# Where the feed-forward's last additions run, and when the third pair's tables are spread: a two-layer attention hybrid on one core

## The chip, the cores and the metric

The kernel runs on one core of one Trainium2 chip. A core has five engines that run side by side, each with its own queue of instructions: TensorE (PE, with PEld for its weight loads) multiplies matrices into PSUM, VectorE (DVE) and ScalarE (ACT) do elementwise work and can read PSUM, GpSimd (POOL) does elementwise work between SBUF tiles, and SyncE (SP) only starts transfers. Transfers (DMAs) are also started from POOL's queue. An instruction waits in its queue until the semaphores it needs have been raised by other engines or by transfers.

The metric is the device time of one execution in microseconds (us); lower is better. Beside it stands the span of a profiled execution, from its first to its last instruction.

## The reference

The input is x, eight images of 32 x 32 positions with 384 channels in fp32. In short:

```python
# layer 0: six heads of 64; scores get two tables of relative positions
x = x + conv_attention(group_norm(x))
#   attn = softmax(q * 64**-0.5 @ k.T + rel_h[:, :, :, :, None] + rel_w[:, :, :, None, :])
#   rel_h = einsum('bhwc,hkc->bhwk', q, Rh),  rel_w = einsum('bhwc,wkc->bhwk', q, Rw)
# layer 1 on the 1024 tokens of an image, one causal head of 384
t = t + causal_attention(layer_norm(t))
# feed-forward, weights reduced to signs, 384 -> 1536 -> 384
t = t + ffn(layer_norm(t))

def quantize(ag):        # one group of images; at both ends of the feed-forward
    gamma = jnp.max(jnp.abs(ag))
    return jnp.clip(ag * QB / (gamma + EPS), -QB + EPS, QB - EPS)     # QB = 128, EPS = 1e-5
```

With eight images and five groups a group is one image, and images 5, 6 and 7 belong to no group: their feed-forward output is zero, so only images 0 to 4 compute it. What the change touches is the last clip with the addition to t behind it, and the way in which the tables rel_h and rel_w reach the score products.

## The kernel before

**Images one after the other.** The loop in `run` takes the images in the order 5, 0, 1, 2, 3, 4, 6, 7. For each it traces layer 0 (`layer0`, with `products` and `attend0_fast`), then layer 1 (`attention1`), then, for images 0 to 4, the feed-forward `ffn`. Neighbouring images overlap: while the feed-forward of one image ends, q of the next is already multiplied (`project_qk`, L505). The last additions of a feed-forward and the output transfers are packed into a function `finish`, put on the list `unfinished`, and called inside the next image's `products`. So there are five joins where a feed-forward's end meets the next image's products: those into images 1, 2, 3, 4 and 6. The joins into images 0 and 7 have none, and image 5 opens the kernel.

**The end of the feed-forward.** The tile y has eight column groups j of 128 x 384. VectorE adds the bias (L1159) and takes maxima (L1160). `absmax_scale` makes one maximum per partition (L1068), POOL takes it over the partitions (`partition_all_reduce`, L1070), and VectorE adds EPS to it (ga, L1071), takes the reciprocal (L1073) and multiplies by 128 (s, L1074). POOL then goes over y: y times s, cut from above (L1164, eight instructions). In `finish` it cuts y from below (L1168) and adds it to xt, the residual (L1169), eight times each; four output transfers follow on POOL's queue (L1224).

**The products of an image.** Three pairs of heads are computed. `queries_keys(m)` copies q of pair m out of PSUM with a bias, one half by ScalarE (L648) and one by VectorE (L646). `positions(p)` multiplies q of pair p with the position tables into four PSUM banks (f_rel, L505), copies them to two pages of SBUF (L666 on ScalarE, L667 on VectorE), writes each page to DRAM (L673) and reads it back in another order into the tile `near` (L678, four reads for each page), all on SP. k and v are made by two `ProductSet`s of fifteen products each, in six PSUM banks A to F (f_pr), whose partial sums ScalarE keeps in pages (L566, L570) and VectorE combines (L585, and L728 for k and L732 for v). All these matmuls are chained by `in_turn`, so TensorE does them in the order of the text.

`place(p)` splits the table of pair p into a rounded part (L693 on ScalarE) and the rest (L703 on VectorE), and then lays both out as the rows f_r that the score products read: sixteen transfers (L708), eight from `pages[0]` on SP and eight from `pages[1]` on POOL. `place(0)` is called in `products`; `place(1)` and `place(2)` come later, from `attend0_fast`.

**The scores.** In `attend0_fast` each pair of heads and each half of the queries has eight rounds of score products: L804 (q times k) and L808 (f_r times `unit`, which adds the positions) go to PSUM, ScalarE takes the exponential (L814), VectorE adds up (L819, L821), and L829 multiplies with v.

**What sets the order.** TensorE's order in the products and scores is written out by hand. On the other engines a planner in the tile framework puts the instructions in a queue order before the kernel runs: it goes through them with estimated durations and takes, whenever an engine is free, the first in the text's order whose inputs it believes to be ready. `tc.issue_after(ins)` makes the instructions of a block on the engine of `ins` stand behind it. PSUM has eight banks of 128 x 512 (`o_tile`), and large SBUF tiles come from pools of ten images and twelve pages: a tile's first write waits for the last reader of whatever held its place.

Of the kernel before, what the change touches and what calls it, by code (L numbers as in the profile page):

```python
# [11 lines left out]
F32 = mybir.dt.float32  # L12
# [3 lines left out]
ALU = mybir.AluOpType  # L16
# [3 lines left out]
P = 128  # L20
# [5 lines left out]
NPAIR = NH // 2  # L26
# [5 lines left out]
QB, QEPS = 128.0, 1e-5  # L32
# [59 lines left out]
def conv_attn_hybrid(  # L92
# [19 lines left out]
    nc = tc.nc  # L112
# [51 lines left out]
    def weight_forms(pools, eng, raw, s):  # L164
# [49 lines left out]
        out=maskT, in_=maskT, compare_op=ALU.is_ge, fill=MASKED, base=0, pattern=[[1, P]], channel_multiplier=-1  # L214
# [13 lines left out]
    for low in (True, False):  # L228

        nc.gpsimd.affine_select(  # L230
            out=over_group, in_=over_group, compare_op=ALU.is_ge, fill=0.0, base=0 if low else NP_GN - 1,
# [142 lines left out]
    def stages(pools):  # L374
# [238 lines left out]
        def layer0(b, xT):  # L613
# [7 lines left out]
            def r(part, p):  # L621
                if not pools.fast:
                    if part not in rooms:
                        rooms[part] = pools.image(f"r_{b}_{part}", F32R)
                    return rooms[part][:, p, :]
                i, at = divmod(4 * (p % 2) + part, NPAIR)
                if i not in rooms:
                    rooms[i] = pools.flat(f"r_{b}_{i}", F32R)
                return rooms[i][:, ts(at, T)]
# [3 lines left out]
            def queries_keys(m):  # L633
                p = m % NPAIR
                bias = bqk[:, m : m + 1]
                made = ahead.pop((b, m)) if (b, m) in ahead else project_qk(b, xT, m, plain[0])
                for half, ps in enumerate(made):
                    t = ts(half, 512)
                    if m < NPAIR:
                        dst = q[:, p, t]  # L640
                    else:
                        dst = k[:, p, t].rearrange("d (g n i) -> d g i n", n=2, i=P)
                        ps = ps.rearrange("d (g i n) -> d g i n", n=2, i=P)
                    scale = qscale if m < NPAIR else 1.0
                    if half and not (pools.fast and b == ORDER[0]):
                        nc.vector.tensor_scalar(dst, ps, scale, bias, ALU.mult, ALU.add)  # L646
                    else:
                        nc.scalar.activation(dst, ps, AF.Identity, bias=bias, scale=scale)  # L648
# [2 lines left out]

            def positions(p):

                room = pools.flat(f"far_{b}_{p}")
                *pages, near = (room[:, ts(i, T)] for i in range(3))
                for half in range(2):
                    ps = [pools.o_tile(f"rel_{b}_{p}_{half}_{par}") for par in range(2)]
                    for par in range(2):  # L660
                        (in_turn if pools.fast else nc.tensor.matmul)(
                            ps[par], rel[rows[par]].rearrange("d a n -> d (a n)"), q[rows[par], p, ts(half, 512)],
                            start=True, stop=True,
                        )
                    for par in range(2):
                        nc.scalar.copy(pages[par][:HD, ts(half, 512)], ps[par][:HD])  # L666
                        nc.vector.tensor_copy(  # L667
                            pages[par].rearrange("i (w h) -> i w h", h=H)[HD:, :, ts(half, H // 2)],
                            ps[par][HD:].rearrange("i (h w) -> i w h", w=W),
                        )  # L670
                for par in range(2):
                    far = store.tile([P, T], F32, tag=f"far_{p}_{par}", bufs=2, name=f"{pools.path}_far_{b}_{p}_{par}")
                    nc.sync.dma_start(out=far, in_=pages[par])  # L673
                    start = far[0:1, 0:1]
                    for d in range(2):
                        for half in range(2):
                            at, step = (d * HD + (half if d else 16 * half)) * T, (2 if d else 1) * T
                            nc.sync.dma_start(  # L678
                                out=near[ts(4 * d + 2 * half + par, 16)].rearrange("m (n o) -> m n o", n=32),
                                in_=bass.AP(start.tensor, start.offset + at, [[step, 16], [T + 32, 32], [1, 32]]),  # L680
                            )
                return near, [page.bitcast(F32R) for page in pages]

            def behind_of(ins):
                return contextlib.nullcontext() if ins is None else tc.issue_after(ins)
# [9 lines left out]
            def place(p, near, pages, behind=(None, None), rounded=False):  # L695

                for d in range(2):
                    hi, lo, src = both(near, pages, d)
                    if not rounded:
                        with behind_of(behind[0]):  # L700
                            round_off(d, near, pages)
                    with behind_of(behind[1]):
                        nc.vector.tensor_tensor(lo, src, hi.bitcast(F32), ALU.subtract)  # L703
                for part in range(4):
                    for d in range(2):
                        for i in range(2):
                            half = part % 2 if d else part // 2
                            (nc.gpsimd if i else nc.sync).dma_start(  # L708
                                out=r(part, p).bitcast(F32).rearrange("(m i) t -> i m t", i=4)[2 * i + d],
                                in_=pages[i][ts(2 * d + 1 - half, 32)].bitcast(F32),  # L710
                            )

            v = pools.flat(f"v0_{b}")[:, : NJ * C].rearrange("p (j c) -> p j c", j=NJ)

# [19 lines left out]
            near = []  # L734

            def products():

                forms = xf.pop(b)
                of_k, of_v = (ProductSet(b, s, forms) for s in (1, 2))
                for m in range(NPAIR):  # L740
                    queries_keys(m)
                    if m:
                        near.append(positions(m - 1))
                of_k.run(5, put_keys)
                near.append(positions(NPAIR - 1))
                if unfinished:
                    unfinished.pop()()
                for d in range(2):
                    of_k.run(3)
                    with behind_of(of_k.last_copy):  # L750
                        of_k.behind = round_off(d, *near[0])
                of_k.run(N_PROD - of_k.at)
                place(0, *near[0], (None, of_k.last_final), rounded=True)
                early = pools.small.tile([P, 1], F32, tag="early", name=f"early0_{b}")
                with behind_of(of_k.last_copy):
                    of_v.behind = nc.scalar.activation(early, of_k.part["n5"][:, 0:1], AF.Exp, scale=0.0).ins
                of_v.run(N_PROD, put_values)
# [307 lines left out]
        def absmax_scale(am, name):  # L1065

            g = pools.small.tile([P, 1], F32, tag="qg", name=f"qg_{name}")
            nc.vector.tensor_reduce(g, am, AX.X, ALU.max)  # L1068
            ga = pools.small.tile([P, 1], F32, tag="qa", name=f"qa_{name}")
            nc.gpsimd.partition_all_reduce(ga, g, P, bass_isa.ReduceOp.max)  # L1070
            nc.vector.tensor_scalar_add(ga, ga, QEPS)  # L1071
            s = pools.small.tile([P, 1], F32, tag="qs", name=f"qs_{name}")
            nc.vector.reciprocal(s, ga)  # L1073
            nc.vector.tensor_scalar_mul(s, s, QB)  # L1074
            return s, ga
# [13 lines left out]
        def ffn(xt, b, gn):  # L1089
# [40 lines left out]
            s, _ = absmax_scale(am.rearrange("p i n -> p (i n)"), f"1_{b}")  # L1130
# [13 lines left out]
            y = pools.flat(f"y2_{b}")[:, : NJ * C].rearrange("p (j c) -> p j c", j=NJ)  # L1144
            am2 = pools.small.tile([P, NJ], F32, tag="am2", name=f"am2_{b}")
            for j in range(NJ):
# [7 lines left out]
                if j == 4:  # L1154
                    xt = pools.flat(f"xagain_{b}")[:, : NJ * C].rearrange("p (j c) -> p j c", j=NJ)
# [2 lines left out]
                    nc.tensor.matmul(ps[:, :C], h, w, start=(i == 0), stop=(i == len(products) - 1))  # L1158
                nc.vector.tensor_tensor(y[:, j, :], ps[:, :C], b2_sb, ALU.add)  # L1159
                nc.vector.tensor_reduce(am2[:, j : j + 1], y[:, j, :], AX.X, ALU.max, apply_absolute_value=True)  # L1160
            s, _ = absmax_scale(am2, f"2_{b}")

            for j in range(NJ):
                nc.gpsimd.tensor_scalar(y[:, j, :], y[:, j, :], s, QB - QEPS, ALU.mult, ALU.min)  # L1164

            def add():
                for j in range(NJ):
                    nc.gpsimd.tensor_scalar_max(y[:, j, :], y[:, j, :], QEPS - QB)  # L1168
                    nc.gpsimd.tensor_tensor(xt[:, j, :], y[:, j, :], xt[:, j, :], ALU.add)  # L1169
                return xt  # L1170

            yield add
# [2 lines left out]
        unfinished = []  # L1175
# [59 lines left out]
    with ExitStack() as scope:  # L1235
        pools = Pools(scope, tc, "f")
# [43 lines left out]
```

## Time and profile before

| What | us |
|---|---|
| median of 3 runs | 2418.41 (2416.07 to 2419.2) |
| the profiled execution, its time | 2416.14 |
| its span, first to last instruction | 2414.4 |
| PE busy | 2327.5 (96%) |
| PEld busy | 1347.2 (56%) |
| DVE busy | 1518.0 (63%) |
| ACT busy | 1090.6 (45%) |
| POOL busy | 566.8 (23%) |

The mean granted TensorE clock is 0.983 of full speed. Busy time is a sum over stages with different limits, and a matmul counts as busy until its modelled end, so PE's 96% doesn't say that every stage is bound by TensorE. The groups of instructions that the change concerns, as mean duration of one in ns and busy time in us over the whole kernel:

| Group | count | mean ns | busy us |
|---|---|---|---|
| L1164 POOL y times s, cut from above | 40 | 1561 | 62.0 |
| L1168 POOL y cut from below | 40 | 1286 | 50.9 |
| L1169 POOL y added to xt | 40 | 1217 | 48.0 |
| L1224 POOL issue of an output transfer | 20 | 771 | 15.4 |
| L708 POOL issue of rows f_r | 192 | 535 | 102.2 |
| L646 DVE copy of q | 21 | 747 | 15.7 |
| L667 DVE copy of f_rel | 96 | 692 | 61.3 |
| L703 DVE rest of the tables | 48 | 1749 | 84.0 |

In the views, a line gives an instruction or a group with what it wrote and read; in square brackets or behind a bar stands how long its engine had been idle before it, and which engine or transfer ended that. A transfer's line is the time of its issue on its queue; it lands some microseconds later (median 3.0 us for rows issued on SP, 4.0 for rows issued on POOL).

### The profile page before, as it was taken

The page shows a single profiled execution, that of the slowest core. Times are in us where ns is not written, and L with a number is a line of the kernel's source. Part 1 is how long each engine was busy: PE and PEld are TensorE (multiplying, and loading weights), DVE is VectorE, ACT ScalarE, POOL GpSimd, SP SyncE. Part 2 cuts the span into 40 slices and gives each one's busy share as a digit, 9 for nine tenths or more (in the row PEclk, how much of TensorE's full clock was granted, in tenths as well). Part 3 has the DMA queues.
Part 4 walks back from the last instruction along what each step waited for, and adds up shares of the span by engine and source line. Part 5 has one row for each costly group of instructions (what it writes and reads, how often), then busy time and mean ns, then how long its engine had stood idle before and what let it go on. Part 6 is the DMA issues. An engine that isn't in the chain of part 4 may idle for free.

```text
span 2414.4 us, 27759 instructions
## 1 busy us (share of the span) xinstructions
PE 2327.5 (96%) x9970; PEld 1347.2 (56%) x9970; DVE 1518.0 (63%) x2364; ACT 1090.6 (45%) x1874; POOL 566.8 (23%) x620
## 2 busy tenths in 40 slices
PE   7999999999899999899998999999999989999998
PEld 4545454568545577445675455864457754555454
DVE  6785578565587346684466864577834668626851
ACT  4552256136463266552465622755424655116520
POOL 4311131020640204411106302063020153021300
PEclk9999999999899999899998999998999989999999
DMA  7430562030730206320217302063102371006200
GB/s 168 136 114 1 160 120 87 14 144 27 139 97 27 79 27 118 110 62 1 105 49 130 84 27 95 35 114 108 43 6 100 75 141 47 27 26 141 69 1 28
DMA packets 156243, 185.83 MB, mean 77 GB/s; under 512 B 113568, under 2 KB 126208, under 8 KB 153280
## 3 DMA queue, kind: packets, MB, share of 16 engines
q1 hardware_dynamic: 135856, 114.66, 20.2%
q0 software_dynamic: 17184, 69.22, 9.1%
q8 instruction: 82, 1.34, 0.2%
q14 instruction: 65, 0.53, 0.1%
q10 hardware_dynamic: 3056, 0.08, 0.1%
HBM read 83.24 MB, written 50.33 MB: 55 GB/s over the span
## 4 chain that ended last, share of the span: by engine, by line
PE 89%; POOL 7%; DMA 2%; DVE 1%; ACT 1%; issue 1%; SPq 0%; POOLq 0%; ACTq 0%
PE f_s L804 14%; PE f_av L829 14%; PE f_s L991 8%; PE f_av L1006 8%; PE f_y L1116 7%; PE f_y L1158 7%; PE f_qk L505 5%; PE f_pj L455 5%; PE f_v L455 5%; PE f_q L950 5%; PE f_s L808 4%; POOL f_y L1164 2%; POOL f_y L1168 2%; POOL f_xagain L1169 2%; PE f_pt L383 1%; PE f_rel L505 1%
## 5 line engine op out<-in xcount | busy, mean ns | idle before, releaser
L814 ACT ACTIVATE f_pr<-f_s 128x512 f32<-128x512 f32 x768 | 413.7, 595 | 134.6 <-PE f_s L808 109.7
L804 PE MATMUL f_s<-f_q,f_k 64*128 64x512 f32 x1536 | 426.5, 617 | 8.5 <-ACT f_pr L814 8.5
L821 DVE TENSOR_TENSOR f_sum<-f_sum,f_pr 128x1024 f32<-128x1024 f32 x288 | 369.9, 1284 | 39.4 <-ACT f_pr L814 18.6
L808 PE MATMUL f_s<-f_r,unit 64*128 64x512 f32 x768 | 334.6, 813 | 42.3 <-DMA f_r<-f_far 42.3
L829 PE MATMUL f_av<-f_pr,f_v 128*64 128x512 f32 x1536 | 339.3, 594 | 0.0
L804 PEld LDWEIGHTS f_s<-f_q,f_k 64*128 64x128 f32 x1536 | 165.3, 192 | 138.8 <-issue 62.3
L829 PEld LDWEIGHTS f_av<-f_pr,f_v 128*64 128x64 f32 x1536 | 106.2, 137 | 196.4 <-issue 191.3
L991 PE MATMUL f_s<-f_q,f_lnT 128*128 128x512 f32 (+3 forms) x576 | 195.9, 488 | 0.0
L1006 PE MATMUL f_av<-f_v,f_pr 128*128 128x385 f32 x576 | 195.3, 486 | 0.0
L708 POOL DMA_DIRECT2D f_r<-f_far x192 | 102.2, 535 | 358.9 <-DVE f_far L703 230.0
L1000 ACT ACTIVATE f_pr<-f_s 128x512 f32<-128x512 f32 (+3 forms) x96 | 46.9, 490 | 279.5 <-DVE f_s L996 233.9
L808 PEld LDWEIGHTS f_s<-f_r,unit 64*128 64x128 f32 x768 | 90.1, 194 | 128.6 <-issue 80.1
L516 POOL TENSOR_TENSOR f_xf<-f_gnT 128x512 f32<-128x512 f32 x28 | 35.5, 1279 | 502.6 <-DVE f_gnT L418 502.6
L1006 PEld LDWEIGHTS f_av<-f_v,f_pr 128*128 128x128 f32 x576 | 108.3, 190 | 77.2 <-issue 11.5
L991 PEld LDWEIGHTS f_s<-f_q,f_lnT 128*128 128x128 f32 x576 | 102.0, 190 | 77.8 <-issue 53.8
L819 DVE TENSOR_TENSOR f_sum<-f_pr,f_pr 128x1024 f32<-128x1024 f32 x48 | 61.0, 1270 | 130.8 <-ACT f_pr L814 130.8
L1158 PE MATMUL f_y<-f_w2a,f_hilo 128*128 128x384 f32 x640 | 128.5, 341 | 5.3 <-DVE f_hilo L1141 5.3
L1127 DVE TENSOR_REDUCE am<-f_h 128x1 f32<-128x1024 f32 (+2 forms) x80 | 71.6, 947 | 96.0 <-ACT f_h L1120 96.0
L505 PE MATMUL f_qk<-f_gnT,wq_sb 128*128 128x512 f32 x288 | 129.5, 601 | 1.7 <-DVE f_gnT L418 1.7
L1120 ACT ACTIVATE f_h<-f_y,b_sb 128x256 f32<-128x256 f32 x240 | 100.6, 471 | 67.4 <-PE f_y L1116 67.4
L950 PE MATMUL f_q<-f_lnT,wqk 128*128 128x512 f32 x288 | 127.5, 592 | 0.0
L455 PE MATMUL f_pj<-wproj_sb,f_oT 128*128 128x384 f32 x384 | 127.3, 488 | 0.0
(213 smaller groups left out, 3708.7 us busy)
## 6 DMA issues: line engine op xcount, KB each, us to landing
f_far<-f_far SPq DMA_DIRECT2D x48, 512.0 KB, 4.2
f_r<-f_far SPq DMA_DIRECT2D x192, 128.0 KB, 3.0
f_r<-f_far POOLq DMA_DIRECT2D x192, 128.0 KB, 4.0
f_gnT<-in_xT SPq DMA_DIRECT2D x24, 512.0 KB, 4.6
f_far<-f_far SPq DMA_DIRECT2D x192, 64.0 KB, 4.6
f_x<-in_x SPq DMA_DIRECT2D x32, 384.0 KB, 6.7
f_w1a<-w1s POOLq DMA_DIRECT2D x5, 1536.0 KB, 6.9
f_w2a<-w2s POOLq DMA_DIRECT2D x5, 1536.0 KB, 9.1
```

Source lines behind the costliest of these rows:

```text
L455: nc.tensor.matmul(ps[:, :C], xT[:, k, ts(j, P)], w[:, k, cols], start=(k == 0), stop=(k == NC - 1))
L505: last_product[0] = nc.tensor.matmul(*args, **kw).ins
L804: nc.tensor.matmul(sc[par], k[rows[par], p, ts(c, P)], q[rows[par], p, ts(half, 512)], start=True, stop=False)
L808: last_matmul[0] = nc.tensor.matmul(sc[par], unit[rows[par], c // 2 % 2].rearrange("i h w -> i (h w)"), r(2 * (c // 4) + c % 2, p)[rows[pa ...
L814: last_exp[0] = nc.scalar.activation(pr[:, ts(par, 512)], sc[par], AF.Exp).ins
L821: adds.append(nc.vector.tensor_tensor(total, total, pr, ALU.add).ins)
L829: last_matmul[0] = nc.tensor.matmul(av[ts(par, HD), :], v[:, c, ts(2 * p + par, HD)], pr[:, ts(par, 512)], start=(c == 0), stop=(c == NJ - 1),
L950: nc.tensor.matmul(ps, wqk[:, k, ts(m, P)], xT[:, half, k, :], start=(k == 0), stop=(k == NC - 1))
L991: nc.tensor.matmul(sc[:, lo:], xT[:, c // 4, k, ts(c % 4, P)], q[:, half, k, lo:], start=(k == 0), stop=(k == NC - 1),)
L1006: nc.tensor.matmul(av[:, : C + 1], prs[c][:, ts(j - c, P)], v[:, c, :], start=(c == 0), stop=(c == j))
L1116: nc.tensor.matmul(ps, w1k[i // 2][:, ts(m, P)], xs[i % 2][:, half, i // 2, :], start=(i == 0), stop=(i == 2 * NC - 1))
L1158: nc.tensor.matmul(ps[:, :C], h, w, start=(i == 0), stop=(i == len(products) - 1))
```

## The change

Three things change.

1. **The clip.** POOL's eight clips take the two bounds at once, before the scale: y is cut to between `low` and `up`, where up = ga (QB - QEPS) / QB and low = -up are two new 128 x 1 values made by VectorE. The scale s is applied in the addition instead.
2. **The additions.** `add` becomes eight `scalar_tensor_tensor` on VectorE (y times s plus xt) in the place of sixteen instructions on POOL. `finish` is called earlier in the text: behind the last `queries_keys` of the next image and ahead of `positions(1)`, where before it came behind `positions(2)`.
3. **The third pair's transfers.** `positions` is divided into `tables` (matmuls and copies) and `spread` (the ten transfers on SP). For pair 2 of the fast path, `tables` stays where `positions` was, and `spread` is traced behind `place(0)`, with an order: SP's eight transfers of rows in `place` stand behind the last transfer of a `spread` traced so far, and pair 2's `spread` stands behind the last of `place(0)`'s eight on SP.

```diff
--- before.py
+++ after.py
@@ -651,7 +651,7 @@
 
 
 
-            def positions(p):
+            def tables(p):
 
                 room = pools.flat(f"far_{b}_{p}")
                 *pages, near = (room[:, ts(i, T)] for i in range(3))
@@ -668,6 +668,12 @@
                             pages[par].rearrange("i (w h) -> i w h", h=H)[HD:, :, ts(half, H // 2)],
                             ps[par][HD:].rearrange("i (h w) -> i w h", w=W),
                         )
+                return pages, near
+
+            sent = [None]
+
+            def spread(p, pages, near):
+
                 for par in range(2):
                     far = store.tile([P, T], F32, tag=f"far_{p}_{par}", bufs=2, name=f"{pools.path}_far_{b}_{p}_{par}")
                     nc.sync.dma_start(out=far, in_=pages[par])
@@ -675,11 +681,14 @@
                     for d in range(2):
                         for half in range(2):
                             at, step = (d * HD + (half if d else 16 * half)) * T, (2 if d else 1) * T
-                            nc.sync.dma_start(
+                            sent[0] = nc.sync.dma_start(
                                 out=near[ts(4 * d + 2 * half + par, 16)].rearrange("m (n o) -> m n o", n=32),
                                 in_=bass.AP(start.tensor, start.offset + at, [[step, 16], [T + 32, 32], [1, 32]]),
-                            )
+                            ).ins
                 return near, [page.bitcast(F32R) for page in pages]
+
+            def positions(p):
+                return spread(p, *tables(p))
 
             def behind_of(ins):
                 return contextlib.nullcontext() if ins is None else tc.issue_after(ins)
@@ -705,10 +714,13 @@
                     for d in range(2):
                         for i in range(2):
                             half = part % 2 if d else part // 2
-                            (nc.gpsimd if i else nc.sync).dma_start(
-                                out=r(part, p).bitcast(F32).rearrange("(m i) t -> i m t", i=4)[2 * i + d],
-                                in_=pages[i][ts(2 * d + 1 - half, 32)].bitcast(F32),
-                            )
+                            with behind_of(None if i else sent[0]):
+                                put = (nc.gpsimd if i else nc.sync).dma_start(
+                                    out=r(part, p).bitcast(F32).rearrange("(m i) t -> i m t", i=4)[2 * i + d],
+                                    in_=pages[i][ts(2 * d + 1 - half, 32)].bitcast(F32),
+                                )
+                            last_put = last_put if i else put.ins
+                return last_put
 
             v = pools.flat(f"v0_{b}")[:, : NJ * C].rearrange("p (j c) -> p j c", j=NJ)
 
@@ -739,18 +751,19 @@
                 of_k, of_v = (ProductSet(b, s, forms) for s in (1, 2))
                 for m in range(NPAIR):
                     queries_keys(m)
+                    if m == NPAIR - 1 and unfinished:
+                        unfinished.pop()()
                     if m:
                         near.append(positions(m - 1))
                 of_k.run(5, put_keys)
-                near.append(positions(NPAIR - 1))
-                if unfinished:
-                    unfinished.pop()()
+                last_tables = tables(NPAIR - 1)
                 for d in range(2):
                     of_k.run(3)
                     with behind_of(of_k.last_copy):
                         of_k.behind = round_off(d, *near[0])
                 of_k.run(N_PROD - of_k.at)
-                place(0, *near[0], (None, of_k.last_final), rounded=True)
+                with behind_of(place(0, *near[0], (None, of_k.last_final), rounded=True)):
+                    near.append(spread(NPAIR - 1, *last_tables))
                 early = pools.small.tile([P, 1], F32, tag="early", name=f"early0_{b}")
                 with behind_of(of_k.last_copy):
                     of_v.behind = nc.scalar.activation(early, of_k.part["n5"][:, 0:1], AF.Exp, scale=0.0).ins
@@ -1158,15 +1171,18 @@
                     nc.tensor.matmul(ps[:, :C], h, w, start=(i == 0), stop=(i == len(products) - 1))
                 nc.vector.tensor_tensor(y[:, j, :], ps[:, :C], b2_sb, ALU.add)
                 nc.vector.tensor_reduce(am2[:, j : j + 1], y[:, j, :], AX.X, ALU.max, apply_absolute_value=True)
-            s, _ = absmax_scale(am2, f"2_{b}")
-
+            s, ga = absmax_scale(am2, f"2_{b}")
+
+            up = pools.small.tile([P, 1], F32, tag="qu", name=f"qu_{b}")
+            nc.vector.tensor_scalar_mul(up, ga, (QB - QEPS) / QB)
+            low = pools.small.tile([P, 1], F32, tag="ql", name=f"ql_{b}")
+            nc.vector.tensor_scalar_mul(low, up, -1.0)
             for j in range(NJ):
-                nc.gpsimd.tensor_scalar(y[:, j, :], y[:, j, :], s, QB - QEPS, ALU.mult, ALU.min)
+                nc.gpsimd.tensor_scalar(y[:, j, :], y[:, j, :], up, low, ALU.min, ALU.max)
 
             def add():
                 for j in range(NJ):
-                    nc.gpsimd.tensor_scalar_max(y[:, j, :], y[:, j, :], QEPS - QB)
-                    nc.gpsimd.tensor_tensor(xt[:, j, :], y[:, j, :], xt[:, j, :], ALU.add)
+                    nc.vector.scalar_tensor_tensor(xt[:, j, :], y[:, j, :], s, xt[:, j, :], ALU.mult, ALU.add)
                 return xt
 
             yield add
```

## The prediction

> **What bounds the kernel now.** I read the page's chain that ended last first, then its costliest groups, the chain around one join between two images, VectorE's and GpSimd's order there, and the same join in an image without feed-forward. From the page:
>
> ```profile
> PE 89%; POOL 7%; DMA 2%; DVE 1%; ACT 1%; issue 1%; SPq 0%; POOLq 0%; ACTq 0%
> L808 PE MATMUL f_s<-f_r,unit 64*128 64x512 f32 x768 | 334.6, 813 | 42.3 <-DMA f_r<-f_far 42.3
> ```
>
> TensorE sets the end except for 7% on POOL. Its one large wait is for the position rows f_r: five waits of 8.0 to 9.1 us, 42.3 in all, one in each image whose products follow a feed-forward (1, 2, 3, 4, 6). I argue in the times of image 4; the others show the same lengths. The chain there, columns start, length, what:
>
> ```profile
> 1593.86 3.22 POOL f_y L1164 x3
> ...
> 1606.25 2.29 POOL f_y L1168 x2
> ...
> 1623.31 2.37 POOL f_xagain L1169 x2
> ...
> 1626.54 2.16 POOL out_y L1224 x3
> 1628.71 4.87 DMA f_r<-f_far
> ...
> 1633.97 0.81 PE f_s L808 x2
> ...
> 1647.52 7.02 PE f_av L829 x32
> ```
>
> Eight clips, sixteen additions' halves and four output issues stand in POOL's queue ahead of the rows that it issues. The timeline of VectorE (start, length, instruction) around that, and one of the wait's ends on TensorE:
>
> ```profile
> 1587.65 0.16 DVE L1073 RECIPROCAL qs<-qa 128x1 f32<-128x1 f32 x1
> 1587.84 0.69 DVE L667 COPY f_far<-f_rel 64x512 f32<-64x512 f32 x1
> 1588.57 0.15 DVE L1074 TENSOR_SCALAR qs<-qs 128x1 f32<-128x1 f32 x1
> ...
> 1592.34 0.75 DVE L646 TENSOR_SCALAR f_q<-f_qk,bqk 128x512 f32<-128x512 f32 x1 [2.28 <-PE f_qk L505]
> ...
> 1625.71 0.69 DVE L732 TENSOR_TENSOR f_v<-f_pr_D,f_u_n 128x512 f32<-128x512 f32 x1 [0.89 <-POOL f_xagain L1169]
> ```
>
> An L667 copy, later in the program's text, stands ahead of L1074: the order on an engine is the planner's, by when it thinks inputs ready, and not the text's. Last, busy times by stretch (us, PE, PEld, DVE, ACT, POOL, PEclk, DMA share, GB/s): behind the wait, and image 7's scores, which follow no feed-forward:
>
> ```profile
> 1633.90:1642.00 8.10, 7.02 (x18) 4.76 (x19) 1.23 (x1) 2.75 (x6) 0.16 (x1) 0.50 0.18 61
> 2208.80:2213.00 4.20, 3.22 (x13) 1.34 (x12) 3.13 (x6) 1.50 (x3) 0.00 (x0) 1.00 0.03 11
> ```
>
> After the wait TensorE ran at clock 0.50 for 8.1 us; image 7 stayed at 1.00.
>
> **What the Trainium skill says.** "TensorE: Matmul & The Clock Gate", What's actually happening: after an idle window of some 3.4 us the array's clock is halved. The trace agrees (0.50 above). Its Architectural detail: VectorE's queue is strictly first in, first out, so an instruction that waits holds all behind it; no row here contradicts that. "GPSIMD Engine Reference", Instruction dispatch: the first call after a library load costs some 6 us. The trace has 5.0: POOL's wait for qs ended at 1588.8, the first clip began at 1593.86. Same page, Key points: POOL shares its SBUF interfaces with VectorE instructions that have two SBUF inputs. L703 beside POOL's additions took 2.47 us each, against 1.62 in image 0's join; beside the clips the effect is small (clips 1.555 to 1.63, one L585 0.97 for 0.69).
>
> **The change, part by part.** *Removed from POOL:* 8 L1168 (50.9/40 = 1.27 us) and 8 L1169 (48.0/40 = 1.20) per image, 19.8 us of the 31.8 from 1593.86 to 1625.68. The rows' issues then wait for L703 instead, as in image 0: L703 ended at 311.6, POOL's issues at 315.6, scores began at 320.1 and no L808 waited. *What returns:* from the first score product to the first L829 image 4 takes 1624.63 to 1647.52 = 22.9 us, image 0 320.13 to 333.32 = 13.2, image 7 2208.88 to 2220.52 = 11.6. Taking the mean of those two, 22.9 − 12.4 = 10.5 us per image: the wait of 8.2 and part of the cold clock.
>
> *Two bounds:* two 128x1 operations, some 0.15 + 0.19 us as L1071 and L1074. The clips no longer need L1073 and L1074, so their start moves by under 0.5 us either way, and POOL is off the path: nothing. Uncovered it would be 5 × 0.4 = 2 us. The clip with two pointer scalars isn't in the trace: at best L1168's uncontended 1.15, at worst 2.0 (half a microsecond for a second pointer); I take L1164's 1.56, ending at 1606.3 (1603 to 1610).
>
> *Eight additions on VectorE:* scalar_tensor_tensor on 128x384. Nearest rows: L1009 617 ns, L1159 558. I take 0.62: 8 × 0.62 = 5.0 us; with L703's slowing (2.47/1.62) at worst 7.6, at best 4.5. VectorE idles about 5.9 us between 1592 and 1608, so the work would fit. The waits may not: addition j can start at 1593.86 + 1.56(j+1), 1595.4 to 1606.3, while the planner, which saw all-reduce to clip without the 5.0 us, expects the first soon after 1590. I expect it to queue each addition 5 to 8 us before its input exists. Behind it wait q's last copy (L646), pair 1's four L667, then L585, pair 2's L667 and L728; for these waits TensorE, by PSUM banks. At 1598 the eight banks hold three products, four of pair 1's f_rel and one of qk's. Pair 2's f_rel matmuls (now 1598.64) need qk's bank and three of pair 1's, product D (1600.56) the fourth.
>
> How late depends on what the planner counts for a clip. L732 tells a little: it was planned behind v's last L585 and waited on POOL's last addition in five of five images, so the planner expected POOL's 24 operations to last until about 1622: (1622 − 1588.7)/24 = 1.39 us. It is weak, since images without POOL work have that order too. Counting 1.2 (additions dearer than clips), I laid the queue out: additions 0 to 2, L646, addition 3, then L667 and additions in turn. In real time addition 2 ends at 1599.1, L646 at 1599.8, the L667 at 1601.4, 1602.9, 1604.5 and 1606.1: D starts 5.5 us late. With 1.4 it is 5.1, with 1.6 2.9, with 1.05 6.3. TensorE works under 2 of 7.5 us there, so a cold spell follows, some 1.2 us. I take 5.3 + 1.2 = 6.5 us late; bounds 0 and 12.
>
> *Table transfers:* spread(2) on SP (2 L673, 8 L678) moves behind place(0)'s eight SP rows. In image 4 four L678 (1615.96 to 1618.5) held 14 rows from 1618.56 on; now the eight go from about 1609, at 0.6 each until 1614. Pair 2's tables are first read about 32 us after place(1) at 1650 (two halves of 16), so their delay of some 10 us is hidden. The rows on SP are hidden as well: POOL's land last. In the three images without feed-forward no L808 waits: nothing. If POOL's cover were gone, SP's rows would be late by 5 us at most.
>
> *Output:* POOL's four L1224 wait for the additions, at worst to 1607, and end by 1611; the rows behind them wait for L703 at about 1620 anyway. Nothing; without that cover it would be the 3.1 us of the four issues.
>
> *Sum:* per image 10.5 − 6.5 = 4.0 us; five times, 20. The profiled execution took 2416.1 us (span 2414.4 and 1.7 around it): 2396. The median of the runs shown lies 2.3 above: **2398 us**.
>
> **The rivals.** *B, the additions fall into VectorE's gaps:* a planner that counts over 2 us per clip, or real clips faster, leaves TensorE undisturbed. For it: 5.9 us idle. Against: the unseen 5.0 us start. 5 × 10.5 = 52, less at most 9: 2366 to 2380, say 2370. *C, slower:* one mechanism, VectorE's queue standing on the clips. If all eight additions are planned ahead of L646, that copy ends at 1607.6, pair 1's fourth L667 at 1610.4, D is 9.9 late; with a cold spell of 1.7 to 3.4 it is 11.6 to 13.3 against 10.5 back: 1 to 3 lost per image, 2424 to 2433, say 2428. It decides once D starts after about 1609; for it speaks that the planner is blind to the start, against it the 1.39. *D, no change:* delay and return cancel, near 2418; or the rows find another late releaser (L703 pushed past 1626), which the same delay of TensorE hides.
>
> **How the numbers follow.** Likeliest 0.52 (2398, own range 2384 to 2410), B 0.20, D 0.10, C 0.18. A difference of 0.2% (5 us) is about what a measurement can tell from none. Faster 0.72 (likeliest and B), same 0.10, slower 0.18. The range 2366 to 2425 leaves out some of B's low end (0.05) and C above 2425 (0.12); it takes in a delay of 0 to 12 us.
>
> **What would show it.** Right: L808 no longer waits on DMA f_r in the five images; POOL busy falls by some 99 us to 468; VectorE rises by 25; new waits of VectorE at the additions on POOL's clips, of 1 us each; f_rel or pr_D on TensorE waits for VectorE's copies, some 5 us per image; clock below 1 there. Wrong: these waits missing (then B), or over 10 us, or L808 still waiting. The prediction falls if the planner's order differs from mine; what I trust least is where the additions stand against L646 and L667.

## The result, and the profile after

The changed kernel takes 2390.57 us (median of 4 runs, 2389.58 to 2396.38) against 2417.24 for the kernel before beside it. The ratio is 0.9894 with a 95% interval of 0.9876 to 0.9912: 26 us, or 1.1%, faster. The profiled execution has a span of 2394.7 us, 19.7 less than before, and a mean clock of 0.989; it is the slowest of the four runs, so it shows less than the 26 us.

From the page of the changed kernel, the chain that ended last, and the score products that add the positions (L808 of the kernel before is L821 now; the clip is L1181, the addition L1185 on VectorE, the issue of the rows L718):

```profile
PE 93%; POOL 2%; DMA 2%; ACT 1%; DVE 1%; issue 1%; SPq 0%; ACTq 0%; DVEq 0%
L821 PE MATMUL f_s<-f_r,unit 64*128 64x512 f32 x768 | 314.6, 801 | 0.0
```

POOL has left the chain but for 2%, and TensorE's 42.3 us of waiting for rows is gone altogether. A smaller wait has taken its place. TensorE's waits, by who ended them (total us, times, longest):

```profile
PE f_rel L505 <- DVE f_far L667: 16.4, 5, 3.4
```

Five times, once in each join, the matmuls of pair 2's tables wait for VectorE's copies of pair 1's. First the kernel before in the join into image 4, the join of the prediction: VectorE's copies of pair 1, TensorE's pair 2 and product D.

```profile
1594.00 2.52 DVE L667 COPY f_far<-f_rel 64x512 f32<-64x512 f32 x4 [0.91 <-ACT f_far L666]
...
1598.64 1.99 PE L505 MATMUL f_rel<-f_q,rel 64*128 64x512 f32 x8
1600.56 1.12 PE L505 MATMUL f_pr_D<-f_gnT,wf 128*128 128x512 f32 x2
```

VectorE in the same join of the changed kernel, where the same instructions stand 12.7 us earlier:

```profile
1579.66 0.75 DVE L646 TENSOR_SCALAR f_q<-f_qk,bqk 128x512 f32<-128x512 f32 x1 [2.17 <-PE f_qk L505]
1581.87 1.56 DVE L1185 SCALAR_TENSOR_TENSOR f_xagain<-f_y,qs,f_xagain 128x384 f32<-128x384 f32 x2 [1.45 <-POOL f_y L1181]
1583.83 0.62 DVE L1185 SCALAR_TENSOR_TENSOR f_xagain<-f_y,qs,f_xagain 128x384 f32<-128x384 f32 x1 [0.40 <-POOL f_y L1181]
...
1588.91 0.62 DVE L1185 SCALAR_TENSOR_TENSOR f_xagain<-f_y,qs,f_xagain 128x384 f32<-128x384 f32 x1 [0.40 <-POOL f_y L1181]
1589.56 2.52 DVE L667 COPY f_far<-f_rel 64x512 f32<-64x512 f32 x4
```

All eight additions stand between q's last copy and pair 1's four copies. The first waits 1.45 us for its clip and most of the others 0.40, and the copies begin at 1589.56 instead of about 1581.3 (1594.00 less 12.7). TensorE and POOL in the same stretch:

```profile
1585.96 1.12 PE L505 MATMUL f_rel<-f_q,rel 64*128 64x512 f32 x2
1590.31 3.78 PE L505 MATMUL f_rel<-f_q,rel 64*128 64x512 f32 x6 [3.23 <-DVE f_far L667]
1594.02 2.07 PE L505 MATMUL f_pr_D<-f_gnT,wf 128*128 128x512 f32 x2
...
1581.18 7.69 POOL L1181 TENSOR_SCALAR f_y<-f_y,qu,ql 128x384 f32<-128x384 f32 x8 [7.00 <-PE f_rel L505]
1588.83 3.08 POOL L1240 DMA_DIRECT2D out_y<-f_xagain  x4
1609.96 0.56 POOL L718 DMA_DIRECT2D f_r<-f_far  x1 [18.04 <-ACT f_u_n L566]
```

TensorE stands still for 3.2 us, and product D takes 2.07 us for two matmuls that took 1.12 before. POOL is idle for 18 us ahead of the rows. The busy times of two stretches, from the gap and from behind it (us, then PE, PEld, DVE, ACT, POOL, PEclk, DMA share, GB/s):

```profile
1586.00:1590.30 4.30, 1.08 (x3) 0.25 (x2) 3.07 (x6) 1.16 (x2) 4.29 (x5) 1.00 0.20 10
1590.30:1597.40 7.10, 7.09 (x11) 3.15 (x12) 5.07 (x8) 1.73 (x3) 1.61 (x3) 0.52 1.00 375
```

The clock is 0.52 for 7.1 us behind the gap, as it was 0.50 behind the wait for rows in the kernel before. By an estimate from these two figures the slow clock costs (1 - 0.52) x 7.1 = 3.4 us here, about as much as the wait itself.

To compare joins I take three distances from each trace's timeline of TensorE, counted from the first f_rel matmul of a join: to product D, to the first score product (L804 in the kernel before, L817 in the changed one), and to the first product with v (L829 and L842). The names of the kernel before are used for all kernels. In the kernel before they are 15.6, 39.65 and 63.1 us, as means of the five joins. Here D comes 6.2 us later, L804 7.3 later, and L829 4.25 us earlier: 6.3, 3.4, 4.7, 2.2 and 4.5 in the five joins, 21.2 together. Elsewhere the span grew by 1.5. So per join the scores gave back 11.6 us (from L804 to L829, 23.4 before and 11.8 after) and the delay in the products took 7.3 of it.

| Busy us | before | after |
|---|---|---|
| PE | 2327.5 | 2332.6 |
| DVE | 1518.0 | 1523.3 |
| ACT | 1090.6 | 1092.3 |
| POOL | 566.8 | 449.5 |

POOL lost 98.9 us of cuts and additions, as counted, and 23.5 more: the clip went from 62.0 us to 38.5. The sum is 122.4, and 5 us came back in POOL's other work. VectorE gained only 5.3 although the additions are 26.4: its subtraction of the tables (L703, now L712) went from 84.0 us to 76.1, and its combining of the pages (L585) lost some 13 more. Both no longer run beside POOL's additions.

### The profile page after: what moved, and what is told of

The parts are those of the page before. It is cut to its first block, busy times and chain, and to the rows that moved or that the text cites. A ratio compares the mean times of both kernels' runs of the same rounds, so it can differ in the third digit from the quotient of the medians.

```text
span 2394.7 us, 27717 instructions
## 1 busy us (share of the span) xinstructions
PE 2332.6 (97%) x9970; PEld 1329.7 (56%) x9970; DVE 1523.3 (64%) x2414; ACT 1092.3 (46%) x1874; POOL 449.5 (19%) x540
## 4 chain that ended last, share of the span: by engine, by line
PE 93%; POOL 2%; DMA 2%; ACT 1%; DVE 1%; issue 1%; SPq 0%; ACTq 0%; DVEq 0%
PE f_s L817 15%; PE f_av L842 14%; PE f_s L1004 8%; PE f_av L1019 8%; PE f_y L1129 7%; PE f_y L1171 7%; PE f_qk L505 5%; PE f_pj L455 5%; PE f_v L455 5%; PE f_q L963 5%; PE f_s L821 4%; PE f_pr_A L505 3%; PE f_pr_B L505 2%; PE f_rel L505 2%; POOL f_y L1181 2%; PE f_pt L383 1%
## 5 line engine op out<-in xcount | busy, mean ns | idle before, releaser
L817 PE MATMUL f_s<-f_q,f_k 64*128 64x512 f32 x1536 | 411.1, 605 | 9.6 <-ACT f_pr L827 9.6
L842 PE MATMUL f_av<-f_pr,f_v 128*64 128x512 f32 x1536 | 339.3, 594 | 0.0
L821 PE MATMUL f_s<-f_r,unit 64*128 64x512 f32 x768 | 314.6, 801 | 0.0
L817 PEld LDWEIGHTS f_s<-f_q,f_k 64*128 64x128 f32 x1536 | 147.5, 188 | 145.0 <-issue 67.7
L842 PEld LDWEIGHTS f_av<-f_pr,f_v 128*64 128x64 f32 x1536 | 106.2, 137 | 196.4 <-issue 192.5
L718 POOL DMA_DIRECT2D f_r<-f_far x192 | 102.2, 535 | 441.4 <-DVE f_far L712 237.7
L821 PEld LDWEIGHTS f_s<-f_r,unit 64*128 64x128 f32 x768 | 77.7, 190 | 91.4 <-issue 91.4
L455 PE MATMUL f_v<-wv_sb,f_lnT 128*128 128x384 f32 x384 | 126.5, 486 | 0.0
```

The source lines that it names most:

```text
L455: nc.tensor.matmul(ps[:, :C], xT[:, k, ts(j, P)], w[:, k, cols], start=(k == 0), stop=(k == NC - 1))
L817: nc.tensor.matmul(sc[par], k[rows[par], p, ts(c, P)], q[rows[par], p, ts(half, 512)], start=True, stop=False)
L821: last_matmul[0] = nc.tensor.matmul(sc[par], unit[rows[par], c // 2 % 2].rearrange("i h w -> i (h w)"), r(2 * (c // 4) + c % 2, p)[rows[pa ...
L842: last_matmul[0] = nc.tensor.matmul(av[ts(par, HD), :], v[:, c, ts(2 * p + par, HD)], pr[:, ts(par, 512)], start=(c == 0), stop=(c == NJ - 1),
```

## The experiments

Four readings of the gain and of the new wait were set against each other.

- *Queue theory* (the prediction's): the rows were late because POOL had the additions ahead of them; now the additions' waits for the clips hold VectorE's queue and take back a part.
- *Work theory*: the part that is lost is the 5 us of additions that VectorE now does, wherever they stand.
- *Transfer theory*: a part of the gain is the new order of SP's transfers.
- *Clip theory*, which the profile after suggests: the clip's new form is itself shorter and makes a part of the gain.

The table has all kernels; the distances are means over the five joins, against the kernel before.

| Kernel | ratio to before, 95% interval | median us | D | L804 | L829 |
|---|---|---|---|---|---|
| the change (e1) | 0.9893 [0.9879, 0.9907] | 2392.9 | +5.8 | +7.4 | -4.5 |
| third part alone (e2) | 0.9987 [0.9978, 0.9995] | 2416.6 | 0.0 | 0.0 | +0.5 |
| without third part (e3) | 0.9909 [0.9896, 0.9922] | 2396.9 | +6.3 | +7.3 | -3.8 |
| old clip, additions moved (e4) | 0.9985 [0.9977, 0.9992] | 2416.4 | +10.8 | +11.8 | -0.5 |
| no clip, additions moved (e5) | 0.9733 [0.9717, 0.9749] | 2354.7 | 0.0 | 0.0 | -12.3 |
| new clip alone, all on POOL (e6) | 0.9798 [0.9774, 0.9823] | 2367.7 | 0.0 | +0.9 | -10.7 |
| behind pair 1's copies (e7) | 0.9739 [0.9723, 0.9755] | 2357.5 | 0.0 | +1.1 | -10.8 |
| behind pair 2's copies (e8) | 0.9743 [0.9726, 0.9759] | 2357.9 | 0.0 | +0.6 | -11.0 |
| old clip, behind pair 2's (e9) | 0.9766 [0.9749, 0.9782] | 2363.9 | 0.0 | +1.7 | -10.2 |
| old clip, bound by pointer (e10) | 1.0008 [0.9999, 1.0017] | 2421.6 | +3.8 | +4.6 | +1.2 |
| both cuts in one, immediates (e11) | 0.9868 [0.9851, 0.9885] | 2387.0 | 0.0 | +1.9 | -7.7 |

The kernel before had medians of 2419.6 beside e1 to e4, 2419.3 beside e5 to e8 and 2420.8 beside e9 to e11.

### The change again, and its third part by itself and taken out (e1, e2, e3)

e1 is the changed kernel. e2 has only the third part: `spread` of pair 2 behind place(0)'s rows; clip, additions and the place of `finish` are those of before. e3 is the change without it:

```diff
-                last_tables = tables(NPAIR - 1)
+                near.append(positions(NPAIR - 1))
...
-                with behind_of(place(0, *near[0], (None, of_k.last_final), rounded=True)):
-                    near.append(spread(NPAIR - 1, *last_tables))
+                place(0, *near[0], (None, of_k.last_final), rounded=True)
```

> The changed kernel again, as the measure for the runs beside it. All theories: 2390 us, give or take 4.

> Only the third part of the change: pair 2's transfers behind place(0)'s rows; clip, additions and their place as before. Queue theory (POOL's rows are late because of the additions, and SP's were hidden behind them): same as before, 2417 +- 4, L808's wait still 8 to 9 us in five joins. Transfer theory (SP's earlier rows carry a part of the gain): at least 10 us faster, 2407 or less.

> The change without its third part: positions(2) undivided and no order on SP's rows. Queue theory: same as the changed kernel, 2390 +- 4. Transfer theory: at least 10 us slower than the changed kernel, 2400 or more.

e1 repeats the result: 0.9893. e2 is 0.13% faster than before, 3 us with an interval of 1 to 5, and its trace still has the whole wait for rows:

```profile
PE f_s L821 <- DMA f_r<-f_far: 45.2, 5, 10.1
```

e3 stands 4 us above e1, with intervals that overlap. The transfer theory falls: SP's order is worth some 3 to 4 us if anything, and nothing of the wait for rows.

### The clip of before under the moved additions (e4)

```diff
-                nc.gpsimd.tensor_scalar(y[:, j, :], y[:, j, :], up, low, ALU.min, ALU.max)
+                nc.gpsimd.tensor_scalar(y[:, j, :], y[:, j, :], s, QB - QEPS, ALU.mult, ALU.min)
...
-                    nc.vector.scalar_tensor_tensor(xt[:, j, :], y[:, j, :], s, xt[:, j, :], ALU.mult, ALU.add)
+                    nc.vector.scalar_tensor_tensor(xt[:, j, :], y[:, j, :], QEPS - QB, xt[:, j, :], ALU.max, ALU.add)
```

> The change with the clip of before on POOL (y times s, cut from above, 1.56 us each) and the cut from below inside VectorE's addition. All eight additions still stand ahead of pair 1's copies. Queue theory (the additions' waits on the clips hold VectorE's queue): the clips end 8 x (1.56 - 0.97) = 4.7 us later, so product D starts 10 to 12 us late instead of 6.1, and five joins lose 24 to 30 us on the changed kernel: 2414 to 2420, about before. Work theory (the 5 us of additions themselves are the delay): D late by 6 as in the changed kernel, 2390 +- 4.

The queue theory's numbers came: D is 10.8 us late, 4.6 more than in the change, and the kernel is back at 0.9985. From the timeline of VectorE, and TensorE's and VectorE's waits (here L1177 is the clip and L1181 the addition):

```profile
1600.54 0.56 DVE L1181 SCALAR_TENSOR_TENSOR f_xagain<-f_y,f_xagain 128x384 f32<-128x384 f32 x1 [0.61 <-POOL f_y L1177]
1601.13 2.52 DVE L667 COPY f_far<-f_rel 64x512 f32<-64x512 f32 x4
...
PE f_rel L505 <- DVE f_far L667: 39.5, 5, 8.2
...
DVE f_xagain L1181 <- POOL f_y L1177: 33.4, 40, 2.7
```

TensorE waits 7.9 us per join for copies that stand behind additions that wait for clips; in the kernel before it waited 8.5 for rows. Moving the additions to this place, with the third part, is worth next to nothing with the old clip. What the change gained, it gained only with the new one.

### No clip, and the new clip alone (e5, e6)

e5 is the change without POOL's eight clips and without the two bounds. e6 is the kernel before, with the new clip and the multiplication in the place of the cut from below:

```diff
-                nc.gpsimd.tensor_scalar(y[:, j, :], y[:, j, :], s, QB - QEPS, ALU.mult, ALU.min)
+                nc.gpsimd.tensor_scalar(y[:, j, :], y[:, j, :], up, low, ALU.min, ALU.max)
...
-                    nc.gpsimd.tensor_scalar_max(y[:, j, :], y[:, j, :], QEPS - QB)
+                    nc.gpsimd.tensor_scalar_mul(y[:, j, :], y[:, j, :], s)
                     nc.gpsimd.tensor_tensor(xt[:, j, :], y[:, j, :], xt[:, j, :], ALU.add)
```

> The change without POOL's eight clips and without the two bounds: the values aren't clipped, the additions take y times s as it is. The eight additions still stand ahead of pair 1's copies, and seven of them ahead of q's last copy too. Queue theory: without the wait on POOL they end 9 us earlier, D is late by under 1 us, and five joins give 11 each: 2355 to 2365. Work theory: D is late by 5 us or more, 2380 to 2390.

> The kernel before with the new clip alone: POOL cuts y by the two bounds, then, in place of the cut from below, multiplies by s and adds, all on POOL. If the clip is 0.59 us shorter and the rest as long as before, POOL ends 4.7 us earlier, L808 waits 3.5 us instead of 8.2, and five joins give 5 to 8 each: 2377 to 2394. If only the additions' move counts, as the prediction has it: 2417 +- 4.

VectorE in e5, in the join into image 4 (L1179 is the addition; the eighth stands just before these seven):

```profile
1550.95 3.79 DVE L1179 SCALAR_TENSOR_TENSOR f_xagain<-f_y,qs,f_xagain 128x384 f32<-128x384 f32 x7
1554.78 0.75 DVE L646 TENSOR_SCALAR f_q<-f_qk,bqk 128x512 f32<-128x512 f32 x1
1555.56 2.52 DVE L667 COPY f_far<-f_rel 64x512 f32<-64x512 f32 x4
```

All eight additions stand ahead of q's last copy here, earlier than in the change, and wait for nothing. They push pair 1's copies by 1.4 us, and D is not late at all. The work theory falls: the same work ahead of the same copies costs nothing where it doesn't wait.

e6 went past both expectations: 2367.7 us, 23 to 25 faster than the whole change. Its groups on POOL (multiplication, addition, clip; busy us, mean ns of one, idle before):

```profile
L1173 POOL TENSOR_SCALAR f_y<-f_y,qs 128x384 f32<-128x384 f32 x40 | 49.3, 1239 | 0.0
L1174 POOL TENSOR_TENSOR f_xagain<-f_y,f_xagain 128x384 f32<-128x384 f32 x40 | 39.0, 993 | 0.0
L1169 POOL TENSOR_SCALAR f_y<-f_y,qu,ql 128x384 f32<-128x384 f32 x40 | 25.7, 650 | 34.8 <-PE f_rel L505 34.8
```

The clip takes 0.65 us here. The 0.97 of the change, from which I expected 4.7 us, is the clip beside VectorE's additions. Per join POOL's work falls from 8 × (1.56 + 1.27 + 1.20) = 32.2 us to 8 × (0.65 + 1.24 + 0.99) = 23.0. That is 9.2 less, 1.7 of it in the additions, which got shorter too. The wait for rows was 8.5, and no L808 waits for rows any more. The additions could have stayed on POOL; moved to where the change puts them, on top of the new clip, they cost the difference between e6 and the changed kernel, 23 to 25 us.

### The additions behind the copies (e7, e8, e9)

The change with `finish` traced behind `positions(1)` (e7) or behind `tables(2)` (e8, e9), and ordered behind the last L667 of those tables, which `tables` keeps in copied[0]; e9 has e4's clip and addition:

```diff
-                    if m == NPAIR - 1 and unfinished:
-                        unfinished.pop()()
...
                 last_tables = tables(NPAIR - 1)
+                if unfinished:
+                    with behind_of(copied[0]):
+                        unfinished.pop()()
```

> The change with the eight additions queued behind pair 1's four L667 (traced behind positions(1), with an order behind its last copy). Queue theory: the copies run on time, pair 2's f_rel waits no more, additions still wait 1 to 3 us for clips and push pair 2's L667 by up to 2 us; D late by under 2 us: 2357 to 2372. Work theory: the 5 us come out later on the path, 2380 to 2390.

> The change with the eight additions queued behind pair 2's four L667, where the clips are done. Queue theory: no wait of VectorE on POOL, D on time; k's L740 come 5 us later, within the 7 us that the banks of v's products leave: 2355 to 2365. Work theory: v's products wait for banks, 2380 to 2390.

> The additions on VectorE behind pair 2's four L667, with the clip of before on POOL. If the place in VectorE's queue decides: the clips end about 4 us after the additions' turn, the additions wait for them and end about 1607, L740 come some 4 us later, within what the banks leave: 2355 to 2375. If the clip's form decides (as the four kernels so far could also be read: the old clip 2416 and 2419, the new one 2355 to 2393): 2400 or more.

All three gave 2357 to 2364 us, as the queue theory had it. In e7 the additions' waits for clips, expected as 1 to 3 us, didn't come, and D is on time. VectorE in e8, the same join (L1186 is the addition):

```profile
1558.02 2.52 DVE L667 COPY f_far<-f_rel 64x512 f32<-64x512 f32 x4 [0.91 <-ACT f_far L666]
...
1564.42 2.52 DVE L667 COPY f_far<-f_rel 64x512 f32<-64x512 f32 x4 [0.35 <-ACT f_far L666]
1566.97 4.32 DVE L1186 SCALAR_TENSOR_TENSOR f_xagain<-f_y,qs,f_xagain 128x384 f32<-128x384 f32 x8
```

The copies run as soon as ScalarE allows, the additions go through in one piece of 4.3 us with no wait, and the later operations on k (L740, L728 of the kernel before) are absorbed: L804 comes 0.6 us late. e9 answers the question that e4 and e6 left together. With the old, long clip the additions wait 4.6 us in all five joins together, and the kernel still gains 2.3%. So the move (with the third part) is worth 57 us (e9) if it stands behind the copies, and the clip by itself 52 us (e6); either of the two is enough to take away the wait for rows, and they don't add up.

e7 and e8 beat both kernels: 2357.5 and 2357.9, a ratio of 0.974 to before, 33 to 35 us below the change. The two can't be told from each other.

### What makes the clip short (e10, e11)

Two kernels with all work on POOL as before. e10 gives the old clip's constant bound by a tile of 128x1 instead of an immediate. e11 multiplies by s first and makes both cuts in one instruction with immediates:

```diff
e10:
+            nc.vector.memset(up, QB - QEPS)
-                nc.gpsimd.tensor_scalar(y[:, j, :], y[:, j, :], s, QB - QEPS, ALU.mult, ALU.min)
+                nc.gpsimd.tensor_scalar(y[:, j, :], y[:, j, :], s, up, ALU.mult, ALU.min)
e11:
-                nc.gpsimd.tensor_scalar(y[:, j, :], y[:, j, :], s, QB - QEPS, ALU.mult, ALU.min)
+                nc.gpsimd.tensor_scalar_mul(y[:, j, :], y[:, j, :], s)
...
-                    nc.gpsimd.tensor_scalar_max(y[:, j, :], y[:, j, :], QEPS - QB)
+                    nc.gpsimd.tensor_scalar(y[:, j, :], y[:, j, :], QB - QEPS, QEPS - QB, ALU.min, ALU.max)
```

> The kernel before, with the clip's upper bound (the constant QB - QEPS) given by a 128x1 tile in place of an immediate; nothing else. If the immediate makes the clip long, it falls from 1.56 to about 0.65 us and the kernel to about 2370. If the operations do (multiply, then minimum), it stays at 1.56 and 2419 +- 4.

> The kernel before, with y times s alone first (one operation) and both cuts in one instruction with two immediates. If the immediate makes a clip long: both cuts take 1.5 us or more, the multiplication 1.24 as measured, 2410 to 2425. If minimum and maximum together are what is short: 0.65 us, POOL ends 7 us earlier, about 2370.

POOL's instructions on y, as shortest, median and longest in ns. First the kernel before, then e10, then e11:

```profile
L1164 POOL TENSOR_SCALAR f_y<-f_y,qs x40: 1555/1556/1630, 608.0 to 1932.3; 128x384 f32<-128x384 f32 x40
L1168 POOL TENSOR_SCALAR f_y<-f_y x40: 1153/1161/2766, 620.4 to 1949.7; 128x384 f32<-128x384 f32 x40
```

```profile
L1167 POOL TENSOR_SCALAR f_y<-f_y,qs,qu x40: 1631/1632/1852, 607.3 to 1936.8; 128x384 f32<-128x384 f32 x40
```

```profile
L1164 POOL TENSOR_SCALAR f_y<-f_y,qs x40: 1232/1234/1250, 607.9 to 1902.1; 128x384 f32<-128x384 f32 x40
L1168 POOL TENSOR_SCALAR f_y<-f_y x40: 499/508/576, 617.8 to 1913.4; 128x384 f32<-128x384 f32 x40
```

The operations decide, not the immediate. Multiply and minimum took 1.56 us, and 1.63 with a second pointer. Minimum and maximum together took 0.51, or 0.65 with two pointers: less than the maximum alone (1.16) or the multiplication alone (1.23).

The totals hold something else besides. e10's 2421.6 came as expected, but its joins into images 1 and 2 are not those of the kernel before: D is 9.1 and 9.7 us late there and on time in the other three. In these two the order on VectorE puts the new memset of the bound's tile between pair 1's copies. In the join into image 2:

```profile
949.21 0.06 DVE L1164 MEMSET qu<- 128x1 f32 x1 [12.08 <-POOL f_y L1167]
949.30 1.30 DVE L667 COPY f_far<-f_rel 64x512 f32<-64x512 f32 x2
...
950.05 2.07 PE L505 MATMUL f_rel<-f_q,rel 64*128 64x512 f32 x2 [7.60 <-DVE f_far L667]
```

An instruction of 0.06 us waits 12 us for POOL's clips, the copies stand behind it, and TensorE stands behind the copies. It is the mechanism of the change with no work in it at all, and it speaks for the queue theory once more.

e11 came out slower than its 2370, at 2387. Its trace is of the fastest of its four runs. Three joins there still wait for rows, 3.6 us together, and in the join into image 2 D starts on time but L804 8.9 us late. A single instruction of VectorE stands behind that:

```profile
942.15 8.46 DVE L585 TENSOR_TENSOR f_u_n<-f_u_n,f_u_n 128x512 f32<-128x512 f32 x1
```

The same instruction takes 0.70 us as a rule (median of this trace). Here it began beside POOL's cuts and additions and ended 0.5 us behind the last of these. ScalarE waited 8.1 us for it, and TensorE then 6.1 us for ScalarE's page copies. Why the other three runs are slower still stays open.

## Why the prediction was right, and where it was right by luck

The time, 2398, lay 7 us above the result. Point by point:

- **The return in the scores**: 10.5 us per join expected, 11.6 measured. The wait for rows went as described, in all five joins; the images without feed-forward have the same distance to L804 as before.
- **The delay in the products**: 6.5 us expected, of it 5.3 of waiting and 1.2 of slow clock. Measured: D 6.2 late, L804 7.3 late, near in sum. The parts are not: TensorE stood for 16.4 / 5 = 3.3 us per join, and the slow clock, which begins ahead of D, is some 3.4 by the estimate above. The wait was smaller than forecast and the clock dearer. The mechanism is the one named: VectorE's queue standing on POOL's clips, which start 7.0 us behind the all-reduce here too. That the order was planned for an earlier start fits this, but no run shows what the planner counted.
- **The sum**: 4.0 us per join expected, 4.25 in the profiled execution.

Besides, two steps of the working were wrong and cancelled.

- "I take L1164's 1.56": the clip of two bounds took 0.97 us beside the additions and 0.65 alone. The stated range (1.15 to 2.0) did not hold it; the half microsecond for a second pointer was 0.08 in e10 (1.63 for 1.56), the rest was bounded by the nearest rows, and no nearest row had minimum and maximum in one instruction. "Two bounds ... nothing" was right of the two small operations and missed what they made possible.
- "additions 0 to 2, L646, addition 3, then L667 and additions in turn": the planner put all eight ahead of pair 1's L667, and none ahead of L646. The 1.39 us drawn from L732's place did not foresee it.

e4 shows the two apart: with the clip at 1.56 us, as I had it, the real queue order makes D 10.8 us late. That is close to rival C's 9.9, and the change comes out at 0.9985 of before. With the additions behind the copies the gain is that of rival B or a little more, whichever the clip (e8, e9). So the forecast's number held, but the sentence behind it, that POOL's lost additions free the rows, describes a gain that this placing doesn't keep unless the clip is shorter too. That is luck.

- **Table transfers**: costed at nothing; 3 to 4 us if anything (e2, e3). The 14 rows named there are six of place(0)'s eight and eight of a later `place`, merged in one line.
- **Two bounds' small operations**: 0.13 and 0.14 us each, and the first clip begins 7.0 us behind the all-reduce as before. Right.
- **Output issues**: hidden; POOL idles 18 us behind them.
- **Busy times**: POOL 449.5 for 468 (the clip again); VectorE +5 for +25, since L703 and L585 lost some 21 us that they had taken longer beside POOL's additions. I had quoted this for L703 and not subtracted it.
- **Rival B's time**, 2370 (2366 to 2380), was meant as what the additions give when nothing holds them. e5, e7 and e8 measured 2355 to 2358: the return was set too low. From L804 to L829 these three give back 11.6 to 12.2 us per join, where 10.5 was taken.

## What to carry to other kernels

Work that is moved to an idle engine is not free because the engine has gaps: ask what it waits for and what stands behind it in that queue. Here the same eight instructions, 5 us of work, cost 7 us of the critical path ahead of four copies and 0.6 us behind them. When several edits come together, run each alone: a number that fits the sum of two wrong terms looks like an understanding. A kernel can also gain by shortening what is waited for (e6), by moving what waits (e8), or by both, with little more. And an instruction that the trace doesn't show is better measured for itself than bounded by its neighbours, if only its operations differ.

## What was not expected of the hardware

- On GpSimd a tensor_scalar of 128x384 in fp32 with minimum and maximum took 0.51 us with immediates and 0.65 with pointers. The maximum alone took 1.16, a multiplication alone 1.23, multiplication with minimum 1.56 to 1.63. Two operations can be less than half of one of them. Why is open.
- Beside each other, one of clip and addition got longer. In the change the clip took 1.03 us (median) where it took 0.65 alone, and VectorE's addition, which reads two SBUF tiles, stayed at 0.62. In e4 the clip stayed at 1.56, and the addition took 0.94 where it took 0.56 alone. The Trainium skill, "GPSIMD Engine Reference", Key points, names interfaces that GpSimd shares with VectorE, with contention where a VectorE instruction has two inputs in SBUF, as here. Beside POOL's work an L585 with two such inputs also took 8.46 us for 0.70 in one join of e11, and 2.5 us in each of the five joins of e6. That the shared interfaces cause these two is likely and was not tested.
- A gap in which TensorE was busy 1.1 of 4.3 us was followed by a clock of 0.52 over the next 7.1 us. TensorE's unbroken idle time ahead of it was 3.1 to 3.4 us in the five joins.
